# Ternary convolution stage: six pairs of x buffers, one padded image, loads five quarters ahead, and an accumulating DMA in place of an add

## The chip, the cores and the metric

The kernel is one program on one core of a Trainium2 chip. The metric is device time of that core in microseconds (us), taken as a median over runs. The engines that matter are TensorE (PE, matmuls), VectorE (DVE), ScalarE (ACT), GpSimd (POOL) and SyncE (SP). SP issues the DMAs that load, POOL issues those that store in the stage concerned. Each engine works through its own queue of instructions in order.

## The reference

Four layers act on x of shape (4, 256, 64, 64) in float32; each adds a convolution of the group-normalised x to x.

```
x = x + L0(gn(x))   # axial attention
x = x + L1(gn(x))   # 3x3 ternary convolution, 256 -> 256
x = x + L2(gn(x))   # two grouped binary 3x3 convolutions with shuffles
x = x + L3(gn(x))   # 3x3 convolution, 256 -> 256
# gn: 32 groups of 8 channels, mean and variance over channels of the group and 64x64
# L1: conv(x, ternize(w, 0.7) * alpha, padding 1) + bias
```

The result of layer 0 isn't formed as one tensor. The attention leaves two outputs in DRAM (called at_d[0] and at_d[1] in the program), each to be scaled per channel, with shifts that are constant per channel. The stage of layer 1 forms x + s0 * at_d[0] + s1 * at_d[1], takes its group statistics, normalises, convolves, and adds the convolution to it.

## The kernel before, in words

The work is one stage per layer. The change lies in the stage of layer 1, lines 1227 to 1418, whose tiles all carry names that begin with d.

**Tiling.** An image b (four of them) is held as two tiles t of 128 channels, and each tile is cut into four quarters q of 16 rows (128 partitions x 1024 elements). Two chunks per quarter compute the two output halves co. 16 quarters make 32 chunks.

**load(b, t, q)** (from L1264) takes a slot for the quarter in row_of (ten slots in five pairs, chosen by (q - b) % 5), issues an SP DMA for the input x into it (L145, in load_shuffled), then two SP DMAs for at_d[1] into a tile "a" (L1276). ACT scales that tile in place (L1279), DVE adds it into the slot (L1281), reading it with its elements in another order. Another SP DMA (L145) brings at_d[0] into another "a" tile, and a DVE scalar_tensor_tensor (L1284) scales and adds it into the slot, with the sum for the statistics as a by-product. ACT squares the slot for the other sum (L1262). There are three "a" buffers.

**norm(b, ts)** turns the sums of a whole image into a scale and a bias per channel: small DVE operations, tiny matmuls (L115, L125, L126) and an ACT operation (L106), one behind the other.

**transform(b, t, q)** writes the normalised quarter and one row of each neighbour into a padded image (ACT, L1322). Tile t has one padded image for interior quarters and one of 19 rows for the edge quarters 0 and 3, whose border rows were set to zero at the start. DVE forms four combinations of rows (L1324, L1328, L1329), ACT casts them to the high part (L1334), and DVE subtracts to get the low part (L1335). High and low parts are double-buffered over quarters.

**chunk(b, q, co)** does 48 matmuls of 128x128 by 128x512 (L1357): four row combinations, two input tiles, high and low part, three column shifts. ACT (L1372) and DVE (L1373, L1374, L1376) combine the four products into 16 rows, DVE adds them into the x slot with the sum for the next layer (L1381), ACT squares (L1262), and POOL issues the stores: x2_d for each chunk (L1386), and z_d for the second half (L1388).

**Order.** Image 0 is loaded and normed first. The loop over quarters then loads quarter q of the next image beside quarter q of this one, and norms the next image after its last quarter. The order on each engine isn't the order of the program text: a planner with priorities interleaves it, and within an engine the queue then runs in order. The next stage (L1420 and on) loads what was stored here, makes padded images (L1553) and row combinations e_tr (L1440), and convolves (L1451). Where a tile of that stage shares its place in SBUF with a tile of this one, it waits for it; the long string of names in the stage's pools sets which lies where.

Of the kernel before, what the change touches and what calls it, by code (L numbers as in the profile page):

```python
# [9 lines left out]
F32 = mybir.dt.float32  # L10
F32R = mybir.dt.float32r
BF16 = mybir.dt.bfloat16
AF = mybir.ActivationFunctionType
ALU = mybir.AluOpType
# [4 lines left out]
P = 128  # L19
B = 4  # L20
C = 256
HW = 4096
# [19 lines left out]
def network(ctx: ExitStack, tc, x, wqkv, relm, relt, relw, relv, counts, masks, vecs, rowv, ab, w1, l2w1, l2w2, l3w, mats, out):  # L42
# [4 lines left out]
    nc = tc.nc  # L47
# [40 lines left out]
    def pool(stack, name, bufs=1, space=None, side=None):  # L88
        kw = {"space": space} if space is not None else {}
        return stack.enter_context(tc.tile_pool(name=name, bufs=bufs, side=side, reuse_waits="tile", **kw))  # L90
# [75 lines left out]
    with ExitStack() as ph:  # L166
# [112 lines left out]
        for b in range(B):  # L279
            xs, gm, rs = ready  # L280
            qs = [qp.tile([P, 8, 8, 64], F32, name=f"qs{t}_{b}", tag="qs") for t in range(2)]
            for k in range(NB):
# [37 lines left out]
                if k % 2 == 1:  # L320
                    for r in range(2):
                        nc.scalar.dma_start(
                            out=vt_d[b][k // 2, r].rearrange("p a c m -> p a (c m)"),
# [8 lines left out]
                if k in (3, 7) and 2 * b + k // 4 - 1 in range(len(pieces)):  # L332
                    i = 2 * b + k // 4 - 1
# [410 lines left out]
    def from_scores(general, keep):  # L744
# [482 lines left out]
        with ExitStack() as ph:  # L1227
            ps_ = {
                k: pool(ph, f"d_{k}", {"a": 3, "o": 2}.get(k, 1))
                for k in "x2 x3 a x4 x5 x0 x6 p2 v0 h00 l00 u0 u1 x1 o s v1 h10 l10 h11 l11 p0 p1 p3 x7 x8 x9 h01 l01".split()  # L1230
            }
# [5 lines left out]

            pads = [
                ps_[f"p{i}"].tile([P, 18 + i // 2, 66], F32, name=f"d_pad{i}", tag="pad") for i in range(4)
            ]  # L1240
            u = [ps_[f"u{t}"].tile([P, 3, 4, C], F32R, name=f"d_u{t}", tag="u") for t in range(2)]
            for t in range(2):
                nc.vector.memset(pads[t][:, :, 0], 0.0)
                nc.vector.memset(pads[t][:, :, 65], 0.0)
                edge = pads[2 + t]
                nc.vector.memset(edge[:, 0:19:18, :], 0.0)
                nc.vector.memset(edge[:, 1:18, 0], 0.0)
                nc.vector.memset(edge[:, 1:18, 65], 0.0)

# [6 lines left out]
            def row_of(b, t, q):  # L1256
                xs[b, t, q] = ps_[f"x{2 * ((q - b) % 5) + t}"].tile([P, HW // 4], F32, name=f"dx_{b}_{t}_{q}", tag="x")
                return xs[b, t, q]
# [5 lines left out]
            def load(b, t, q):  # L1264
# [9 lines left out]
                for two in range(2):  # L1274
# [3 lines left out]
                    )  # L1278
                nc.scalar.activation(a, a, AF.Copy, scale=prs[t, 1][:, 0:1])  # L1279
                xv = xt.rearrange("p (n k i) -> p n k i", k=4, i=16)  # L1280
                nc.vector.tensor_tensor(xv, a.rearrange("p (k n i) -> p n k i", k=4, i=16), xv, ALU.add)  # L1281
                a = ap_.tile([P, HW // 4], F32, name=f"a0_{b}_{t}_{q}", tag="a")
# [26 lines left out]
            def transform(b, t, q):  # L1309


                nb, ra = norms[b, t]
                edge = q in (0, 3)
                pad = pads[2 + t if edge else t]
                pad = pad[:, 1:19] if q == 3 else pad[:, 0:18]
                parts = [(xs[b, t, q].rearrange("p (h w) -> p h w", w=64), slice(1, 17))]
# [88 lines left out]
            norm(0, slice(1, 2))  # L1405
            transform(0, 1, 0)
            for b in range(B):
                for q in range(4):
                    if b + 1 < B:
                        for t in range(2):  # L1410
                            load(b + 1, t, q)
                        if q == 3:
                            norm(b + 1, slice(0, 2))
                    nxt = (b, q + 1) if q < 3 else (b + 1, 0)
                    for co in range(2):
                        if nxt[0] < B:
                            transform(nxt[0], co, nxt[1])
                        chunk(b, q, co, b == q == co == 0)
            lost = None
            if not general:  # L1420
# [470 lines left out]
```

## Time and profile before

| what | value |
|---|---|
| time, median of 3 runs | 2771.07 us (2767.38 to 2775.86) |
| the profiled execution's own time | 2766.54 us |
| its span | 2764.8 us |
| mean granted TensorE clock | 0.937 |
| PE busy | 2398.3 us, 87% |
| DVE busy | 1980.3 us, 72% |
| ACT busy | 1205.8 us, 44% |
| POOL busy | 105.4 us, 4% |
| first matmul of the stage | 1485.0 us |
| last matmul of the stage starts | 1908.9 us |
| first matmul of the next stage's convolution | 1919.09 us |

The times of one execution come from its trace, in us from the span's start. A group line gives the line in the program, the engine, the operation, the output and input tiles, the count, then busy time and mean ns of one, and last the idle time of the engine just ahead of these instructions with what ended it ("<-"). SPq is the queue of DMAs that SyncE issues. A window line gives the busy time and the count of each engine in a stretch of time, then the granted clock, the share of the core's 16 DMA engines that was busy, and GB/s. Some matmul records can be missing from a trace, a few per cent.

### The profile page before, as it was taken

The numbers are of one execution on the slowest core, as the hardware profiler recorded it, in microseconds if no ns is written. First come the engines' busy times: TensorE is split into PE (matmuls) and PEld (weight loads), VectorE is DVE, ScalarE is ACT, GpSimd is POOL, SyncE is SP. The second block draws the span as 40 slices with busy tenths as digits, with TensorE's granted clock in tenths as the row PEclk, the third lists the DMA queues.
The fourth block names the chain that finished last, engine by engine and source line by source line (L and its number), as shares of the span: only waits on it lengthen the run. The fifth ranks groups of instructions, "written<-read, shape, count | busy, mean of one in ns | idle before, by whom it ended". The sixth has DMA issues, their size and how long they took to land.

```text
span 2764.8 us, 78125 instructions
## 1 busy us (share of the span) xinstructions
PE 2398.3 (87%) x34632; PEld 1576.4 (57%) x34632; DVE 1980.3 (72%) x3362; ACT 1205.8 (44%) x1984; POOL 105.4 (4%) x201
## 2 busy tenths in 40 slices
PE   7999788888997888888773998998979859999998
PEld 4566555556665666666662776776545424444443
DVE  6665788988775466666558788885888877967742
ACT  4555355555555544555435466553448421110100
POOL 0000100000001000000000000000000000000000
PEclk9999899999999888899886999999989979999999
DMA  6766366666667777778776546524337742324110
GB/s 239 258 201 205 89 190 163 172 168 186 155 150 159 244 251 249 256 242 274 232 234 220 186 154 201 189 101 158 126 128 265 288 159 91 138 105 137 46 42 36
DMA packets 287996, 489.87 MB, mean 177 GB/s; under 512 B 32736, under 2 KB 149088, under 8 KB 274848
## 3 DMA queue, kind: packets, MB, share of 16 engines
q1 hardware_dynamic: 224992, 359.52, 42.9%
q10 hardware_dynamic: 48256, 58.73, 6.2%
q0 software_dynamic: 14400, 66.53, 6.1%
q8 instruction: 273, 4.47, 0.7%
q14 instruction: 75, 0.61, 0.1%
HBM read 281.46 MB, written 203.23 MB: 175 GB/s over the span
## 4 chain that ended last, share of the span: by engine, by line
issue 38%; PE 30%; DVE 14%; DMA 11%; ACT 5%; POOL 1%; SPq 1%; DVEq 0%; ACTq 0%; POOLq 0%
PE pd L505 5%; PE dc L1357 4%; PE po L293 3%; PE pv L308 3%; PE pq L526 3%; DMA at_d<-o_False 2%; PE e_False L867 2%; DMA x<-x_d 2%; PE pr_False L936 2%; DVE pt L877 2%; PE pe_False L970 2%; DMA dx<-in_x 2%; PE den_False L918 2%; PE pa_False L945 2%; PE pc L1451 2%
## 5 line engine op out<-in xcount | busy, mean ns | idle before, releaser
L1066 PE MATMUL gc<-gtr,g_u 128*128 128x512 f32 x1152 | 503.4, 599 | 11.3 <-DVE gtr L1044 6.7
L1066 PEld LDWEIGHTS gc<-gtr,g_u 128*128 128x128 f32 x1152 | 219.3, 191 | 287.3 <-issue 269.4
L512 DVE STREAM_TRANSPOSE t<-pd 128x1024 f32<-128x1024 f32 x256 | 304.5, 1229 | 86.0 <-PE pd L505 80.7
L505 PE MATMUL pd<-rm,qb 64*32 64x256 f32 x8192 | 305.5, 389 | 41.4 <-DVE t L512 32.3
L1451 PE MATMUL pc<-e_tr,e_k 128*64 128x512 bf16 x2304 | 265.3, 391 | 20.5 <-DVE e_tr L1440 13.3
L532 ACT ACTIVATE o<-pq 128x512 f32<-128x512 f32 x256 | 150.6, 594 | 267.0 <-PE pq L526 264.8
L1357 PE MATMUL dc<-dh,d_u 128*128 128x512 f32 x768 | 233.5, 414 | 33.9 <-ACT dh L1334 33.8
L505 PEld LDWEIGHTS pd<-rm,qb 64*32 64x32 f32 x8192 | 168.4, 108 | 134.7 <-DVE t L512 57.4
L907 ACT ACTIVATE pt<-pt,sm 128x512 f32<-128x512 f32 x256 | 162.7, 710 | 174.9 <-DVE pt L877 174.8
L1357 PE MATMUL dc<-dl,d_u 128*128 128x512 f32 x768 | 229.3, 408 | 0.4 <-DVE dl L1335 0.2
L1451 PEld LDWEIGHTS <-e_k 128*64 128x64 bf16 x2304 | 145.5, 112 | 137.2 <-issue 28.9
L526 PEld LDWEIGHTS pq<-t,t 64*64 64x64 f32 x8192 | 146.0, 138 | 86.1 <-issue 71.6
L526 PE MATMUL pq<-t,t 64*64 64x64 f32 x8192 | 168.5, 225 | 28.6 <-issue 23.5
L1357 PEld LDWEIGHTS dc<-dh,d_u 128*128 128x128 f32 x768 | 148.6, 195 | 74.9 <-ACT dh L1334 35.8
L877 DVE TENSOR_TENSOR pt<-e_False,si_False 128x1024 f32<-128x1024 f32 x128 | 151.6, 1216 | 34.6 <-PE e_False L867 34.3
L1357 PEld LDWEIGHTS dc<-dl,d_u 128*128 128x128 f32 x768 | 145.7, 191 | 42.2 <-DVE dl L1335 4.1
L1084 ACT COPY gc_c<-gc 128x512 f32<-128x512 f32 x32 | 18.6, 582 | 344.0 <-PE gc L1066 344.0
L867 PE MATMUL e_False<-qc_False,rw 32*128 32x256 f32 x1024 | 131.1, 481 | 27.4 <-DVE pt L877 15.8
L538 ACT ACTIVATE sq<-o 128x1024 bf16<-128x1024 f32 x128 | 135.5, 1059 | 4.0
L293 PE MATMUL po<-xg,wt 128*128 128x512 f32 x256 | 120.8, 611 | 6.1 <-DVE st L300 4.5
L970 PE MATMUL pe_False<-pt,ve 128*32 128x64 f32 x4096 | 91.4, 244 | 39.9 <-issue 31.8
L308 PE MATMUL pv<-wt,xg 128*128 128x256 f32 x512 | 120.0, 382 | 0.0
(403 smaller groups left out, 3604.5 us busy)
## 6 DMA issues: line engine op xcount, KB each, us to landing
si_False<-qk_d SPq DMA_DIRECT2D x64, 1024.0 KB
qk_d<-o SPq DMA_DIRECT2D x496, 128.0 KB
x<-x_d SPq DMA_DIRECT2D x32, 1056.0 KB
xa<-in_x SPq DMA_DIRECT2D x16, 1024.0 KB
vt_d<-vs ACTq DMA_DIRECT2D x32, 512.0 KB
q_d<-qs SPq DMA_DIRECT2D x64, 256.0 KB
qb<-q_d SPq DMA_DIRECT2D x128, 128.0 KB
qc_False<-q_d SPq DMA_DIRECT2D x64, 256.0 KB
```

The costliest lines, as they stand in the source:

```text
L293: nc.tensor.matmul(psf, lhsT=wt[:, t, bass.ts(o, P)], rhs=xg[:, t, :], start=(t == 0), stop=(t == 1))
L308: nc.tensor.matmul(pv[:, j, :], lhsT=xg[:, t, pix], rhs=wt[:, t, C : 2 * C], start=(t == 0), stop=(t == 1),)
L505: nc.tensor.matmul(pds[t][32 * c : 32 * c + 32, m].rearrange("p j k -> p (j k)"), lhsT=q[rows, 2 * (gp % 2) + g, a, 32 * nb : 32 * nb + 32 ...
L512: nc.vector.transpose(ts[t][:, :, 32 * jh : 32 * jh + 32].rearrange("p a j b -> p j a b"), pds[t].rearrange("p m j k -> p j m k"),)
L526: nc.tensor.matmul(ps[nb][64 * g : 64 * g + 64, m, :], lhsT=ts[1][rows, n // 2, :, n % 2], rhs=ts[0][rows, n // 2, :, n % 2], start=True, ...
L532: nc.scalar.activation(o[:, :, n : n + 8, :], ps[nb].rearrange("p n (a b) -> p a n b", b=2), AF.Copy, accum_out=acc[:, nb, gp, col : col + 1],
L867: nc.tensor.matmul(es[x_ // 2][:, x_ % 2, :, :, par], lhsT=rw[rows, 63 - i : 127 - i].rearrange("p j r -> p (j r)"), rhs=q[rows, :, par, k ...
L877: nc.vector.tensor_tensor(dst, e, src, ALU.add)
L907: nc.scalar.activation(s, s, AF.Exp, scale=s2q[:, gp : gp + 1])
L1066: nc.tensor.matmul(ms[k], lhsT=u[t][:, dx, k, bass.ts(co, P)], rhs=vs[t][:, k, :, dx : dx + 64], start=(first and dx == 0), stop=(last and ...
L1357: nc.tensor.matmul(at[k], lhsT=u[t][:, dx, k, bass.ts(co, P)], rhs=v[:, k, :, dx : dx + 64], start=(first and p_ == 0 and dx == 0), stop=( ...
L1451: nc.tensor.matmul(m[64 * g : 64 * g + 64], lhsT=parts[:, g, i, k, dx, :], rhs=vs[g][:, k, 8 * (q % 2) : 8 * (q % 2) + 8, dx : dx + 64], s ...
```

## The change

Four things change together.

- The x slots become twelve in six pairs, chosen by (4b + q) % 6, so that the quarters of all images form one ring. To fit, the four padded images become two of 18 rows, one for each tile, which all quarters share; an edge quarter first sets its border row to zero with a DVE memset. The "a" buffers become four, and the tiles' order in SBUF is another.
- ACT no longer scales at_d[1] in place but writes another "a" tile, called ad, in the order that the slot has.
- The DVE add of that tile into the slot is gone. In its place POOL issues a DMA that adds ad into the slot (accum_op), SBUF to SBUF, 32 in all.
- The loop loads five quarters ahead: the first quarter of image 1 before the loop, then one tile of quarter n + 5 after each chunk of quarter n. The norm of the next image comes after its last quarter's load, one quarter earlier than before.

```diff
--- before.py
+++ after.py
@@ -1226,8 +1226,8 @@
 
         with ExitStack() as ph:
             ps_ = {
-                k: pool(ph, f"d_{k}", {"a": 3, "o": 2}.get(k, 1))
-                for k in "x2 x3 a x4 x5 x0 x6 p2 v0 h00 l00 u0 u1 x1 o s v1 h10 l10 h11 l11 p0 p1 p3 x7 x8 x9 h01 l01".split()
+                k: pool(ph, f"d_{k}", {"a": 4, "o": 2}.get(k, 1))
+                for k in "x2 x3 a x4 x5 x0 x6 p0 v0 h00 l00 u0 u1 x1 o s v1 h10 l10 h11 l11 x7 x8 x9 p1 x10 x11 h01 l01".split()
             }
             ap_, op, sp = ps_["a"], ps_["o"], ps_["s"]
             wide = pool(ph, "d_ps3", 1, PSUM)
@@ -1235,17 +1235,11 @@
             ring = [pool(ph, "d_ps", 2, PSUM)] * 2 + [wide]
             taken = [0]
 
-            pads = [
-                ps_[f"p{i}"].tile([P, 18 + i // 2, 66], F32, name=f"d_pad{i}", tag="pad") for i in range(4)
-            ]
+            pads = [ps_[f"p{t}"].tile([P, 18, 66], F32, name=f"d_pad{t}", tag="pad") for t in range(2)]
             u = [ps_[f"u{t}"].tile([P, 3, 4, C], F32R, name=f"d_u{t}", tag="u") for t in range(2)]
             for t in range(2):
                 nc.vector.memset(pads[t][:, :, 0], 0.0)
                 nc.vector.memset(pads[t][:, :, 65], 0.0)
-                edge = pads[2 + t]
-                nc.vector.memset(edge[:, 0:19:18, :], 0.0)
-                nc.vector.memset(edge[:, 1:18, 0], 0.0)
-                nc.vector.memset(edge[:, 1:18, 65], 0.0)
 
             def load_weights(t):
                 for dx in range(3):
@@ -1254,7 +1248,7 @@
             xs, vs, sums, mvs, norms, shift = {}, {}, {}, {}, {}, {}
 
             def row_of(b, t, q):
-                xs[b, t, q] = ps_[f"x{2 * ((q - b) % 5) + t}"].tile([P, HW // 4], F32, name=f"dx_{b}_{t}_{q}", tag="x")
+                xs[b, t, q] = ps_[f"x{2 * ((4 * b + q) % 6) + t}"].tile([P, HW // 4], F32, name=f"dx_{b}_{t}_{q}", tag="x")
                 return xs[b, t, q]
 
             def square(src, out):
@@ -1276,9 +1270,12 @@
                     nc.sync.dma_start(
                         out=a[two:P:2].rearrange("p (k f) -> p k f", k=4), in_=src[:, :, bass.ts(q, 256)]
                     )
-                nc.scalar.activation(a, a, AF.Copy, scale=prs[t, 1][:, 0:1])
-                xv = xt.rearrange("p (n k i) -> p n k i", k=4, i=16)
-                nc.vector.tensor_tensor(xv, a.rearrange("p (k n i) -> p n k i", k=4, i=16), xv, ALU.add)
+                ad = ap_.tile([P, HW // 4], F32, name=f"ad_{b}_{t}_{q}", tag="a")
+                nc.scalar.activation(
+                    ad.rearrange("p (n k i) -> p n k i", k=4, i=16), a.rearrange("p (k n i) -> p n k i", k=4, i=16),
+                    AF.Copy, scale=prs[t, 1][:, 0:1],
+                )
+                nc.gpsimd.dma_start(out=xt, in_=ad, accum_op=ALU.add)
                 a = ap_.tile([P, HW // 4], F32, name=f"a0_{b}_{t}_{q}", tag="a")
                 load_shuffled(a, at_d[0][b][bass.ts(t, P), bass.ts(q, HW // 4)], 0)
                 nc.vector.scalar_tensor_tensor(
@@ -1310,9 +1307,9 @@
 
 
                 nb, ra = norms[b, t]
-                edge = q in (0, 3)
-                pad = pads[2 + t if edge else t]
-                pad = pad[:, 1:19] if q == 3 else pad[:, 0:18]
+                pad = pads[t]
+                if q in (0, 3):
+                    nc.vector.memset(pad[:, 0 if q == 0 else 17, :], 0.0)
                 parts = [(xs[b, t, q].rearrange("p (h w) -> p h w", w=64), slice(1, 17))]
                 if q > 0:
                     parts.append((xs[b, t, q - 1][:, 15 * 64 :].rearrange("p (h w) -> p h w", w=64), slice(0, 1)))
@@ -1404,18 +1401,20 @@
             load_weights(1)
             norm(0, slice(1, 2))
             transform(0, 1, 0)
+            for t in range(2):
+                load(1, t, 0)
             for b in range(B):
                 for q in range(4):
-                    if b + 1 < B:
-                        for t in range(2):
-                            load(b + 1, t, q)
-                        if q == 3:
-                            norm(b + 1, slice(0, 2))
                     nxt = (b, q + 1) if q < 3 else (b + 1, 0)
+                    far = divmod(4 * b + q + 5, 4)
                     for co in range(2):
                         if nxt[0] < B:
                             transform(nxt[0], co, nxt[1])
                         chunk(b, q, co, b == q == co == 0)
+                        if far[0] < B:
+                            load(far[0], co, far[1])
+                    if far[0] < B and far[1] == 3:
+                        norm(far[0], slice(0, 2))
             lost = None
             if not general:
                 far = small(keep, [P, 1])
```

## The prediction

> **What bounds the kernel now.** I read the page's totals, then the stage of the ternary convolution (about 1485 to 1918 us, the only one edited) by 20 us windows, the timeline where a window is low, and last groups and SyncE waits.
>
> ```profile
> PE 2398.3 (87%) x34632; PEld 1576.4 (57%) x34632; DVE 1980.3 (72%) x3362; ACT 1205.8 (44%) x1984; POOL 105.4 (4%) x201
> ...
> q0 software_dynamic: 14400, 66.53, 6.1%
> ...
> L1357 PE MATMUL dc<-dh,d_u 128*128 128x512 f32 x768 | 233.5, 414 | 33.9 <-ACT dh L1334 33.8
> ```
>
> The convolution is 2 x 768 matmuls at L1357, 48 per chunk (one quarter, one output half), 32 chunks. Most of PE's idle time before them (33.8 us) is ended by ACT's cast L1334, the end of an input transform. Windows (PE busy and count, PEld, DVE, ACT, POOL, PE clock, DMA share, GB/s):
>
> ```profile
> 1480.00:1500.00 20.00, 10.44 (x30) 7.47 (x30) 19.86 (x22) 15.73 (x21) 0.00 (x0) 0.67 0.69 213
> 1500.00:1520.00 20.00, 7.28 (x20) 5.43 (x21) 14.91 (x31) 14.49 (x21) 0.00 (x0) 0.53 0.56 180
> 1600.00:1620.00 20.00, 14.10 (x50) 10.43 (x49) 17.29 (x32) 17.73 (x24) 1.06 (x2) 0.83 0.29 94
> 1620.00:1640.00 20.00, 20.00 (x87) 15.84 (x87) 17.77 (x29) 12.69 (x16) 0.53 (x1) 1.00 0.55 171
> 1700.00:1720.00 20.00, 12.54 (x49) 9.01 (x47) 18.33 (x44) 16.73 (x23) 1.06 (x2) 0.83 0.43 135
> 1800.00:1820.00 20.00, 14.00 (x53) 10.27 (x51) 16.42 (x42) 15.34 (x20) 1.59 (x3) 0.83 0.08 35
> ```
>
> Streaming, PE is the bound: 87 matmuls in 20 us, 0.230 us each, 11.0 us per chunk. At the three image boundaries only 50, 49 and 53 issue:
>
> ```profile
> 1608.53 2.50 PE L1357 MATMUL dc<-dh,d_u 128*128 128x512 f32 x5 [5.70 <-ACT dh L1334]
> ...
> 1712.88 2.93 PE L1357 MATMUL dc<-dh,d_u 128*128 128x512 f32 x6 [6.49 <-ACT dh L1334]
> ...
> 1814.44 2.92 PE L1357 MATMUL dc<-dh,d_u 128*128 128x512 f32 x6 [5.70 <-ACT dh L1334]
> ```
>
> These are three lines of the timeline; the bracket is PE's idle time and what ended it. The next image's statistics come after its last load: around 1594 the last L1284, then square, norm (1596.7 to 1601.7), pad and transform (1602.1 to 1608.5), while PE runs dry. Groups of the loads, window 1480 to 1910, and SyncE's waits, 1440 to 1920:
>
> ```profile
> L1284 DVE SCALAR_TENSOR_TENSOR dx<-a,sm,dx 128x1024 f32<-128x1024 f32 x28 | 35.9, 1282 | 0.2
> L1281 DVE TENSOR_TENSOR dx<-a,dx 128x1024 f32<-128x1024 f32 x28 | 34.3, 1224 | 19.4 <-issue 10.2 <-DMA dx<-in_x 8.3 <-ACT a L1279 0.7
> L1279 ACT ACTIVATE a<-a,sm 128x1024 f32<-128x1024 f32 x27 | 31.0, 1148 | 34.6 <-DMA a<-at_d 22.5 <-issue 12.0
> ```
> ```profile
> SPq L145 <- DVE dx L1281: 127.4, 23, 15.5
> ...
> SPq L145 <- DMA x_d<-dx: 46.4, 8, 16.8
> ...
> SPq L145 <- DMA z_d<-dx: 31.0, 10, 14.4
> ```
>
> An x load waits until the chunk that used its slot has stored the result (x_d, z_d). In the timeline, L1381 starts at 1641.38, the stores issue at 1642.90 and 1643.42, the x load at 1649.12, and the add L1281 starts at 1653.00: 11.6 us. For the other tile 1654.15, 1660.75, 1664.79: 10.6 us.
>
> **What the Trainium skill says.** "Collectives: The Full Stack", The bandwidth ceiling: the fold count and why AG ≠ RS ≠ AR: a DMA that adds needs two source reads, the addition itself is not the cost. "DMA: Bandwidth & Descriptors", Anatomy of one DMA, SWDGE path: about 2.0 us plus bytes at 436 GB/s; for 0.524 MB that is an estimate of 3.2 us, and x_d's landings here are 2.8 to 5.1, median 3.0 us, so it agrees. Twice the data term gives an estimate of 4.4 us for the accumulate; no trace of before has one. The same page, Issuing engines are not separate DMA queues: all issuers share 16 DMA engines. The trace's shares include every queue and allow such a sum.
>
> **The change part by part.**
>
> *Five quarters ahead, sixth pair.* The last quarter of the next image is loaded and normed one quarter (two chunks, 22 us) earlier. In the compiled order the norm's PE matmuls move from the last chunk before the boundary to three quarters through the one before it. Gain: three windows hold 152 matmuls, worth 152 x 0.230 = 35 us of their 60, so 25 us; the pure idle is 5.70 + 6.49 + 5.70 = 17.9, and the rest is slow restarting at clock 0.83. I take -24 (bounds -17.9, -25). Left over: at the first boundary the last load's L1284 stands in DVE's order only 7.3 us of work after the L1381 that frees its slot, ahead of the norm's operations; I estimate 4 us of PE stall there and at the second together (0 to 8).
>
> *DVE adds to DMAs.* 32 x 1.22 = 39 us of DVE work goes, 16 border memsets of about 0.1 us (128x66; nearest row, 128x1 at 0.15) come. Between first and last L1381 DVE has 312.9 us of work before and, with the trace's durations on the new order, 290.4 after: 9.7 per chunk instead of 10.4, against PE's 11.0. While PE streams that is worth nothing.
>
> *What the accumulate adds to the chain.* x load, ACT scale, accumulate, L1284 replace x load, add, L1284. From L1381 to L1284: 11.6 + about 0.6 issue (stores: 0.533) + landing 4.4 = 16.6 us. The order leaves on average 14.9 us of DVE work between the two (10.5 before to the add), which at PE's pace is 14.9 x 11.0 / 9.7 = 16.9 us. So it just fits. Beyond that each load stalls DVE, behind which the transforms and evictions queue, and PE waits for those: the chunk takes L / 1.54, as 14.9 / 9.7 = 1.54 chunks lie between. L = 17 costs nothing, 18 gives 11.7 us (+0.7), 19 gives 12.3 (+1.3), for 20 refills: 0, +14, +27 us. Single distances run from 7 to 20, so some stalls come even at 16.6; I take +5 (0 to +30).
>
> *POOL's queue.* It becomes store, accumulate, store, z store, accumulate. An accumulate waits there for the x load into the slot just stored, and the next chunk's store is queued behind; that store's slot waits in turn. One round is 9.4 + 0.5 for one tile and 10.3 + 0.5 for the other = 20.7 us, against 22.0 per quarter: hidden, with 1.3 us to spare. Longer landings come out of this margin, priced in the same +5.
>
> *DMA.* One copy of 0.524 MB costs q0's rate: 0.061 x 2764.8 x 0.524 / 66.53 = 1.33 us of all 16 engines. With two reads up to 2.7; two per 22 us quarter adds 0.12 to 0.24 to a share of 0.55 in the streaming window. Below full, so a lengthening only.
>
> *SP and ACT at the start.* The a0 load waits for the buffer of an earlier accumulate (four "a" buffers) and the next a1 stands behind it in SP's queue. For the second tile's norm (1502 us before) I estimate 3 us later; bounds +10, and -5 because DVE was 19.86 of 20 us busy in 1480 to 1500 and loses four adds of 1.22 there. ACT's permuted scale: same 1.15 us taken; if twice, ACT is at 12.69 of 20 while streaming and hides 32 x 1.15.
>
> *Shared pad.* Tile t's transforms already follow one another on ACT and DVE, so no new wait that binds: zero; if its readers were late, one pad copy (1.25 us) for each of 12 edge quarters inside the stream, which DVE's 1.3 us slack per chunk covers. Dropped setup memsets: hidden under the layer before.
>
> *Tail.* Tiles moved in SBUF: the next layer's first e_tr now lies over the last quarter's x tile and must wait for its stores (last issue 1913.86, z_d landing median 4.5, so about 1918.5) before its transform of 0.7 us pieces; PE restarted at 1919.09. I take +3 (1 to 6).
>
> Sum: -24 + 4 + 5 + 3 + 3 = -9. On the profiled execution (2766.54 us, span 2764.8) that is 2757.5; the median shown, 2771.07, is 4.5 above it, so I predict 2762 as median. Runs differ by 0.15% around it; 0.3%, 8.3 us, is what a measurement here can tell from no change.
>
> **Rivals.**
>
> *The accumulate sets the pace (slower).* Place: L1284 on DVE, waiting for a POOL DMA. For it: 16.6 against 16.9 us is no margin, DMA gets busier, POOL has 1.3 us. Against: a load now runs over three quarters before its transform, so only DVE's order, never missing data, can make PE wait, and distances average out. With 7 us landing L is 19.2, 12.5 us per chunk, 20 x 1.5 = +30, less the 24 saved, plus 10 elsewhere: 2771 + 16 = 2787. It decides for slower from L = 18.5 (12.0; +20 against the other -14, so +6) to 18.7 (above +8).
>
> *Full gain.* The accumulate lands like a store (3.2 us), DVE's freed time shortens start and boundaries: -24 + 0 - 2 + 1 + 2 = -23: 2748. For: the saturated start. Against: the first boundary's 7.3 us.
>
> *Boundaries only shifted.* If the last load's refill is late by the 10 us that a blocked POOL queue costs, norm comes late again and half of the 24 returns: -12 + 12 = 0, 2771. For: the norm sits behind L1284 in DVE's order. Against: it moved a whole chunk ahead.
>
> **How the numbers follow.** Forecast 0.44, of it 0.33 below 2763 and 0.11 above (own range 2752 to 2768); full gain 0.12; shifted 0.12 (0.10 same, 0.02 slower); accumulate pace 0.32 (0.31 slower, 0.01 same). So faster 0.45, same 0.22, slower 0.33. Range 2747 to 2790: it cuts about one in ten on each side.
>
> **What would show it.** Right: windows at the boundaries with over 75 matmuls; L1284 with idle time below 10 us ended by the accumulate; accumulate landings of 4 to 5 us. Wrong: L1284's idle over 20 us, POOL stores waiting for x loads longer than 2 us, streaming windows below 80 matmuls, or the first convolution chunk more than 10 us later.

## The result and the profile after

The change made the kernel slower: 2786.73 us median (2781.4 to 2793.16, 6 runs) against 2768.7 us (2760.02 to 2775.86, 6 runs); ratio 1.0062, 95% interval 1.004 to 1.0083. The profiled execution has a span of 2779.5 us, against 2764.8 before.

From the page after: the totals, the queue that POOL issues into, and the convolution's first group.

```profile
PE 2395.8 (86%) x34632; PEld 1582.8 (57%) x34632; DVE 1944.2 (70%) x3340; ACT 1204.8 (43%) x1984; POOL 133.5 (5%) x233
...
q0 software_dynamic: 19008, 83.31, 9.3%
...
L1354 PE MATMUL dc<-dh,d_u 128*128 128x512 f32 x768 | 235.0, 415 | 14.8 <-ACT dh L1331 14.3
```

The 33.8 us that PE stood before the convolution's matmuls waiting for ACT's cast have become 14.3, and DVE has 36 us less work. Both are what the change set out to do, and the kernel is slower. The windows of the stage (the same columns as before the change) show where PE stands now.

```profile
1540.00:1560.00 20.00, 20.00 (x85) 15.65 (x85) 11.34 (x17) 8.74 (x12) 1.50 (x3) 1.00 0.91 257
1560.00:1580.00 20.00, 19.49 (x82) 15.09 (x81) 15.75 (x24) 10.77 (x11) 3.38 (x5) 1.00 0.85 239
1580.00:1600.00 20.00, 7.82 (x33) 5.83 (x31) 7.27 (x18) 6.71 (x12) 2.85 (x4) 0.83 0.94 282
1600.00:1620.00 20.00, 19.37 (x73) 15.50 (x74) 15.34 (x38) 13.18 (x19) 1.44 (x2) 0.83 0.54 166
...
1700.00:1720.00 20.00, 13.01 (x46) 10.23 (x45) 8.18 (x28) 7.37 (x13) 2.80 (x4) 0.74 0.77 206
1800.00:1820.00 20.00, 17.27 (x64) 13.51 (x63) 13.15 (x41) 9.89 (x14) 1.06 (x2) 0.83 0.13 54
```

Away from the boundaries PE still issues 82 to 88 matmuls in most windows. The stalls are still three, one for each image, but they come earlier, and the DMA share just ahead of the first is 0.85 to 0.94. In the timeline after, they end at another instruction:

```profile
1600.63 0.59 PE L115 MATMUL pst<-sm,mt 128*128 128x2 f32 x2 [12.81 <-DVE sm L1295]
...
1709.50 0.59 PE L115 MATMUL pst<-sm,mt 128*128 128x2 f32 x2 [6.99 <-DVE sm L1295]
...
1808.26 0.59 PE L115 MATMUL pst<-sm,mt 128*128 128x2 f32 x2 [2.73 <-DVE sm L1295]
```

L115 is the first tiny matmul of norm. It stands in PE's queue inside a chunk, and PE takes its queue in order: all convolution matmuls behind it wait until the statistics of the next image are there, that is, until its last load is. Before the change, PE ran dry because the transform came late (17.9 us in all). Now it is held by the norm matmul (12.81 + 6.99 + 2.73 = 22.5 us), because the loads come late. Ahead of the first stall, POOL gets to an accumulate only when the x load has landed, and DVE then stands for that accumulate:

```profile
1589.05 0.87 POOL L1278 DMA_DIRECT2D dx<-ad  x1 [2.70 <-DMA dx<-in_x]
...
1591.10 1.28 DVE L1281 SCALAR_TENSOR_TENSOR dx<-a,sm,dx 128x1024 f32<-128x1024 f32 x1 [7.47 <-DMA dx<-ad]
```

Groups after (window 1470 to 1930) and SyncE's waits (1440 to 1940) show the loads of the whole stage:

```profile
L1281 DVE SCALAR_TENSOR_TENSOR dx<-a,sm,dx 128x1024 f32<-128x1024 f32 x28 | 35.9, 1283 | 69.8 <-DMA dx<-ad 46.1 <-issue 21.6 <-DMA a<-at_d 2.1
...
L1278 POOL DMA_DIRECT2D dx<-ad x28 | 24.3, 869 | 254.1 <-ACT ad L1274 89.6 <-DMA dx<-in_x 85.1 <-ACT dh L1331 21.9
```
```profile
SPq L1270 <- DMA dx<-ad: 85.2, 13, 8.6
SPq L145 <- DMA dx<-ad: 80.6, 13, 10.3
```

Three waits around the accumulate are visible: DVE's L1281 for its landing (46.1 us), POOL's own queue for the x load (85.1), and SyncE's loads for an "a" buffer that an accumulate still reads (85.2 + 80.6 = 166). They are called the slot chain, POOL's order and the ring below. The DMA view of the stream (1520 to 1850), first before and then after, gives the landings in us, last column.

```profile
x_d<-dx POOLq DMA_DIRECT2D x26, 512.0 KB, 3.0
...
z_d<-dx POOLq DMA_DIRECT2D x13, 512.0 KB, 4.7
```
```profile
x_d<-dx POOLq DMA_DIRECT2D x25, 512.0 KB, 5.3
dx<-ad POOLq DMA_DIRECT2D x22, 512.0 KB, 5.4
...
z_d<-dx POOLq DMA_DIRECT2D x12, 512.0 KB, 6.8
```

**Where the 15 us lie.** The chunks' last DVE step (L1381 before, L1378 after) gives three lengths from one line of each trace: when the first runs, how long from first to last, and how long from the last to the next layer's first convolution matmul (1919.09 us before, 1934.37 after). What follows that matmul takes 842 to 851 us in every trace of this study but doesn't belong to the change.

```profile
L1381 DVE SCALAR_TENSOR_TENSOR dx<-dc_o,dx x32: 1215/1221/1227, 1528.2 to 1911.8; 128x1024 f32<-128x1024 f32 x32
```
```profile
L1378 DVE SCALAR_TENSOR_TENSOR dx<-dc_o,dx x32: 1201/1219/1226, 1529.1 to 1923.5; 128x1024 f32<-128x1024 f32 x32
```

The first result is 0.9 us later, the stream of 383.6 us becomes 394.4 (+10.8), the tail of 7.3 becomes 10.9 (+3.6). The sum is 15.3.

The 0.9 us hide something. When the first chunk runs depends on when the layer before ends, too, and that scatters: its last store of at_d[1] (L985) is issued between 1441.0 and 1470.4 us in the twenty traces of this study, though no edit touches that layer. Before and after:

```profile
L985 ACTq DMA_DIRECT2D at_d<-o_False x32: 326/326/1017, 971.8 to 1459.4; - x32
```
```profile
L985 ACTq DMA_DIRECT2D at_d<-o_False x32: 326/326/920, 970.7 to 1446.3; - x32
```

From that store to the first L1381 or L1378 it is 68.8 us before and 82.8 after. This length, called the start below, repeats well: it is 82.8 and 83.0 us in two kernels with the same start (after, g3_start_only), and 66.6 and 66.4 in two others (e13_add_a3, e11_traffic), whose first chunks are 17.2 us apart. So inside the stage the start is 14.0 us longer, the stream 10.8 and the tail 3.6, which makes 28.4; the layer before happened to end 13.1 us earlier. The medians differ by 18 us. The lengths are of one execution each, so part of the 28.4 may be scatter.

### The profile page after: what moved, and what is told of

It is laid out like the page before. It is cut to its first block, busy times and chain, and to the rows that moved or that the text cites. A ratio compares the mean times of both kernels' runs of the same rounds, so it can differ in the third digit from the quotient of the medians.

```text
span 2779.5 us, 78149 instructions
## 1 busy us (share of the span) xinstructions
PE 2395.8 (86%) x34632; PEld 1582.8 (57%) x34632; DVE 1944.2 (70%) x3340; ACT 1204.8 (43%) x1984; POOL 133.5 (5%) x233
## 5 line engine op out<-in xcount | busy, mean ns | idle before, releaser
L1066 PE MATMUL gc<-gtr,g_u 128*128 128x512 f32 x1152 | 504.2, 600 | 11.1 <-DVE gtr L1044 6.7
L1450 PE MATMUL pc<-e_tr,e_k 128*64 128x512 bf16 x2304 | 264.8, 391 | 22.2 <-DVE e_tr L1439 12.1
L1354 PE MATMUL dc<-dh,d_u 128*128 128x512 f32 x768 | 235.0, 415 | 14.8 <-ACT dh L1331 14.3
L1450 PEld LDWEIGHTS <-e_k 128*64 128x64 bf16 x2304 | 154.2, 112 | 129.9 <-issue 29.6
L945 PE MATMUL pa_False<-pt,vb 128*32 128x64 f32 x4096 | 97.9, 235 | 22.7 <-issue 15.4
```

The costliest lines, as they stand in the source:

```text
L1066: nc.tensor.matmul(ms[k], lhsT=u[t][:, dx, k, bass.ts(co, P)], rhs=vs[t][:, k, :, dx : dx + 64], start=(first and dx == 0), stop=(last and ...
L1354: nc.tensor.matmul(at[k], lhsT=u[t][:, dx, k, bass.ts(co, P)], rhs=v[:, k, :, dx : dx + 64], start=(first and p_ == 0 and dx == 0), stop=( ...
L1450: nc.tensor.matmul(m[64 * g : 64 * g + 64], lhsT=parts[:, g, i, k, dx, :], rhs=vs[g][:, k, 8 * (q % 2) : 8 * (q % 2) + 8, dx : dx + 64], s ...
```

## The experiments

The table gives each run's ratio to the kernel before and, from its profile (one execution each), when the first chunk's last step runs, and the lengths of start, stream and tail, all in us.

| run | ratio, 95% interval | first | start | stream | tail |
|---|---|---|---|---|---|
| before | 1 | 1528.2 | 68.8 | 383.6 | 7.3 |
| after | 1.0062 (1.004 to 1.0083) | 1529.1 | 82.8 | 394.4 | 10.9 |
| e1_add | 0.9868 (0.9817 to 0.9919) | 1518.8 | 59.2 | 361.8 | 8.5 |
| e2_acc_only | 1.029 (1.0243 to 1.0337) | 1566.8 | 96.4 | 438.5 | 7.3 |
| e3_copy | 0.9968 (0.9934 to 1.0003) | 1532.7 | 73.9 | 373.0 | 10.8 |
| e4_norm_late | 1.008 (1.0063 to 1.0098) | 1533.5 | 80.8 | 390.8 | 11.2 |
| e5_ad_own | 1.0117 (1.0081 to 1.0152) | 1551.3 | 103.6 | 387.4 | 10.9 |
| e6_side | 1.0057 (1.0039 to 1.0075) | 1542.0 | 82.4 | 389.1 | 11.1 |
| e8_stores_act | 1.01 (1.0071 to 1.0128) | 1535.7 | 81.0 | 406.3 | 9.2 |
| e9_old_loop | 0.9841 (0.98 to 0.9883) | 1510.8 | 62.4 | 358.7 | 8.4 |
| e13_add_a3 | 0.9925 (0.9881 to 0.9968) | 1533.3 | 66.6 | 363.6 | 14.6 |
| e11_traffic | 0.9944 (0.9923 to 0.9966) | 1516.1 | 66.4 | 377.6 | 8.6 |
| e14_small | 0.9924 (0.9902 to 0.9946) | 1510.1 | 69.1 | 364.9 | 10.8 |
| e1b_add_ad | 0.989 (0.9846 to 0.9935) | 1517.6 | 66.5 | 369.4 | 9.1 |
| g1_ring5 | 1.0105 (1.0084 to 1.0127) | 1529.8 | 82.4 | 392.2 | 11.1 |
| g2_side5 | 1.006 (1.0032 to 1.0087) | 1542.5 | 80.2 | 387.4 | 10.9 |
| g3_start_only | 0.9964 (0.9942 to 0.9986) | 1539.1 | 83.0 | 358.9 | 8.2 |
| g4_add5 | 0.9883 (0.9854 to 0.9912) | 1508.9 | 57.0 | 366.1 | 8.3 |
| h1_ring5_act | 1.0149 (1.0111 to 1.0187) | 1535.5 | 83.2 | 401.9 | 8.9 |
| h2_side5_act | 1.0065 (1.0037 to 1.0093) | 1525.3 | 82.4 | 391.9 | 8.5 |

### Is it the accumulate? (e1_add, e2_acc_only, e4_norm_late)

e1_add keeps the whole change but the accumulating DMA (this diff is shortened; "permuted" stands for the reordered view):

```diff
-                ad = ap_.tile(..., tag="a")
-                nc.scalar.activation(ad (permuted), a (permuted), AF.Copy, scale=prs[t, 1][:, 0:1])
-                nc.gpsimd.dma_start(out=xt, in_=ad, accum_op=ALU.add)
+                nc.scalar.activation(a, a, AF.Copy, scale=prs[t, 1][:, 0:1])
+                nc.vector.tensor_tensor(xv, a.rearrange("p (k n i) -> p n k i", k=4, i=16), xv, ALU.add)
```

> The changed kernel with the accumulating DMA taken out: ACT scales the tile in place and DVE adds it into the slot, as before; six pairs, shared pads, four a buffers and loads five quarters ahead stay. Theory A (the accumulate in the chain from store to L1281 makes the last load of an image late, and PE's small norm matmuls wait for it): the three boundary stalls of 12.8, 7.0 and 2.7 us go, PE gaps of the stage below 3 us in all, and the time is 15 to 25 us below the kernel before, about 2748 us. Theory B (the earlier norm itself, or the store and load chain through six slots, stops PE whatever does the add): gaps over 8 us stay at the boundaries, time 2765 us or more.

e2_acc_only makes the opposite edit on the kernel before, and nothing else.

> The kernel before with nothing changed but the add: ACT writes a second a tile and POOL accumulates it by DMA; five pairs, four pads, three a buffers and the old loop stay. Theory A: the old loop has only 10.5 us of DVE work between freeing and refilling a slot, so each refill stalls DVE by about 16.6 - 12 = 4 us or more: 24 refills, +40 us or more at the most, at least +15 us, so 2785 to 2815 us. Theory B: the accumulate is hidden also here, within 6 us of the kernel before.

e4_norm_late keeps the accumulates and moves norm and the next image's first transform behind the first chunk of the last quarter:

```diff
+                        if q == 3 and co == 0:
+                            chunk(b, q, co)
+                            if nxt[0] < B:
+                                norm(nxt[0], slice(0, 2))
                         if nxt[0] < B:
                             transform(nxt[0], co, nxt[1])
-                        chunk(b, q, co, b == q == co == 0)
+                        if q < 3 or co == 1:
+                            chunk(b, q, co, b == q == co == 0)
...
-                    if far[0] < B and far[1] == 3:
-                        norm(far[0], slice(0, 2))
```

> The changed kernel with norm and the first transform of the next image put after the first chunk of an image's last quarter instead of ahead of it; accumulates stay. PE's small norm matmuls then stand at 7.0, 15.0 and 23.0 chunks instead of 6.6, 14.7 and 22.5, so 4.2, 3.0 and 5.3 us later. Theory A (the loads are late): the stall at the first boundary falls from 12.8 to about 9 us, at the second from 7 to 4, the third vanishes, unless the transform behind it is now late: 2776 to 2784 us. Theory B (placement alone): stalls gone, 2755 to 2768 us.

e1_add is 1.3% faster than the kernel before, more than theory A expected. e2_acc_only is 2.9% slower, 2856 us and so well beyond what either theory expected. So the accumulate, with the third tile ad that it needs, costs about (1.0062 - 0.9868) x 2769 = 54 us in the changed kernel and 80 us in the old one. By lengths, the changed kernel stands above e1_add by 23.6 us in the start, 32.6 in the stream and 2.4 in the tail. The windows of e1_add at the places where PE stood:

```profile
1580.00:1600.00 20.00, 20.00 (x86) 15.72 (x85) 17.76 (x33) 14.15 (x19) 0.53 (x1) 1.00 0.39 129
1600.00:1620.00 20.00, 20.00 (x89) 15.90 (x88) 18.05 (x37) 13.35 (x20) 1.59 (x3) 1.00 0.63 206
1680.00:1700.00 20.00, 17.15 (x71) 12.75 (x70) 19.91 (x34) 16.60 (x23) 1.05 (x2) 1.00 0.33 118
1780.00:1800.00 20.00, 18.84 (x81) 14.37 (x80) 20.00 (x29) 14.04 (x18) 1.05 (x2) 1.00 0.13 52
```

The first boundary is gone, the others lose 4 us of PE between them, the clock stays at 1.00. DVE is at 18 to 20 of 20 us here, with the adds still on it, and that costs little: the stream is 21.8 us shorter than before (361.8 against 383.6). e4_norm_late moved part of the stall from L115 (7.4 and 3.3 us) to the transform behind it (3.1 and 3.2) and gained nothing (1.008; its median of 2793 us is above what both theories gave). Where the norm stands is not the cause, so theory B of that run is out; late loads remain.

### Which other part of the change gains? (e9_old_loop, e13_add_a3, g4_add5)

e9_old_loop is e1_add with the loop of the kernel before:

```diff
-            for t in range(2):
-                load(1, t, 0)
...
+                    if b + 1 < B:
+                        for t in range(2):
+                            load(b + 1, t, q)
+                        if q == 3:
+                            norm(b + 1, slice(0, 2))
...
-                        if far[0] < B:
-                            load(far[0], co, far[1])
-                    if far[0] < B and far[1] == 3:
-                        norm(far[0], slice(0, 2))
```

> The run with the DVE add (six pairs, shared pads, four a buffers, no accumulate) with the loop of the kernel before: next image's quarter q loaded beside this one's, norm in the same quarter. In the compiled order PE's norm matmuls stand at 6.65, 15.3 and 22.9 chunks all the same. If the sixth pair of slots makes the loads early and the planner does the rest, within 6 us of the run with the new loop: 2730 to 2746 us. If the new loop's order makes the gain, the boundary stalls return in part: 2750 to 2770 us.

It is as fast (0.9841, stream 358.7). The last load is summed (L1278, the L1284 of before) 242.5 us after the first chunk's result, in e1_add 237.0 and before the change 271.8: the planner takes the loads ahead by itself. So the early loads and the vanished boundaries need no "five quarters ahead", which adds nothing that these runs can tell. They come with the six pairs and the shared pads that make room for them; no run separates these two, nor the new order of the tiles in SBUF.

e13_add_a3 is e1_add with three a buffers (`-{"a": 4` `+{"a": 3`).

> The run with the DVE add with three a buffers instead of four, as the kernel before had. If two tiles per load need no fourth buffer: within 6 us of it, 2728 to 2744 us; else up to 2760 us. It is also the control for the run with bare traffic.

g4_add5 is e9_old_loop with `{"a": 5}` and one buffer for the tile o.

> The candidate for a version faster than both: DVE add, six pairs, shared pads, the old loop, five a buffers and one o buffer. Four buffers against three went with 15 us. If a fifth still lets SyncE's queue run further ahead at the start and in the stream: 2720 to 2732 us; if four were enough: as the run with the old loop, 2728 to 2738 us; if the single o buffer binds: over 2745 us.

With three buffers the start takes 66.6 us, with four 59.2, and the stream is nearly the same (363.6 and 361.8). The fourth buffer's gain, 0.6% with intervals that overlap, lies in the start (7.4 us) and the tail (6.1) if it is real. A fifth, at the price of the second o buffer, gave nothing more: against e9_old_loop the start is 5.4 us shorter and the stream 7.4 longer.

### Bytes or waits? (e3_copy, e14_small, e11_traffic, e1b_add_ad, e6_side)

e3_copy is a plain copy in the same place with the same waits:

```diff
-                nc.gpsimd.dma_start(out=xt, in_=ad, accum_op=ALU.add)
+                nc.gpsimd.dma_start(out=xt, in_=ad)
```

> The changed kernel with the POOL DMA a plain copy instead of an accumulate, in the same place of every queue with the same waits; the input x is left out of the sum, since the copy overwrites it. If the second source read is what costs (DMA engines 75 to 94% busy in the stretches before the stalls): landings fall from 5.4 to about 3 to 4 us, the DMA share by about 0.12, and at least half of the 18 us goes: 2765 to 2778 us. If the cost is the chain and the queues themselves (POOL waits for the x load, SyncE for the a buffer, whatever the transfer's rate): 2780 to 2788 us.

About half of the 54 us goes ((1.0062 - 0.9968) x 2769 = 26 us). The landing falls from 5.4 to 4.1 us. Queue q0 was busy 7.7% of 2761.3 us here, 9.3% of 2779.5 after and 6.3% of 2733.0 in e1_add: one copy costs (212.6 - 172.2) / 32 = 1.3 us of all 16 DMA engines, one accumulate (258.5 - 172.2) / 32 = 2.7 us. (This is the time that the packets took, in this traffic; the percentages are rounded, so each figure is good to about 0.1 us.)

e6_side keeps the traffic and POOL's instructions, but aims the accumulate beside the sum:

```diff
-                nc.gpsimd.dma_start(out=xt, in_=ad, accum_op=ALU.add)
+                nc.gpsimd.dma_start(out=a, in_=ad, accum_op=ALU.add)
+                nc.vector.tensor_tensor(xt, ad, xt, ALU.add)
```

> The changed kernel with its accumulates aimed beside the sum: POOL accumulates ad into the a tile that ACT has read already (nothing reads it again), and DVE adds ad into the slot as in the run without accumulates. DMA traffic, POOL's instructions and the buffers held until landing stay; the slot and L1281 no longer wait for the accumulate, nor the accumulate for the x load. If the chain through the slot is the cost: within 15 us of the run with the DVE add, 2735 to 2750 us. If the DMA traffic and the held buffers are: 2760 to 2785 us.

No slot waits for an accumulate here, and the time is that of the changed kernel (1.0057). So L1281's wait, the largest wait of DVE in the profile after, is not needed for the loss. The held buffers aren't quite those of the changed kernel, though: here the a tile is held until the landing beside ad. SyncE waits 101.8 + 28.9 = 130.7 us for accumulates.

e14_small accumulates 16 of the 1024 columns, otherwise as e6_side:

```diff
-                nc.gpsimd.dma_start(out=a, in_=ad, accum_op=ALU.add)
+                nc.gpsimd.dma_start(out=a[:, 0:16], in_=ad[:, 0:16], accum_op=ALU.add)
```

> The run with the accumulate beside the sum, with 16 of the 1024 columns accumulated instead of all: every wait and held buffer stays, with the landing's fixed part alone (2 to 3 us), and 1/64 of the traffic. If the bytes are the cost: within 10 us of the run with the DVE add, 2730 to 2748 us. If the held buffers and the order of the queues are the cost whatever is moved: 2765 us or more.

e1b_add_ad has the third tile and DVE's add, and no DMA:

```diff
-                nc.gpsimd.dma_start(out=xt, in_=ad, accum_op=ALU.add)
+                nc.vector.tensor_tensor(xt, ad, xt, ALU.add)
```

> The changed kernel with three tiles per load in the ring of four a buffers as there, ad written by ACT, and DVE adding ad into the slot; no DMA in its place. Against the run with the DVE add it has only the third tile: if the ring with three tiles is tight by itself, 2750 us or more; if it is tight only because a tile is held until an accumulate lands, within 8 us of it, 2726 to 2746 us.

It gives 0.989 against 0.9868, with intervals that overlap; start and stream are 7.3 and 7.6 us longer. So the third tile alone may be worth some 6 us of the 54, and it is the nearer control for e6_side and e14_small.

e11_traffic is the run with three buffers and DVE's add (e13_add_a3), plus accumulates into an added scratch tile that nothing waits for:

```diff
                 nc.scalar.copy(hi, v)
+                if 1 <= 4 * b + q <= 11:
+                    nc.gpsimd.dma_start(
+                        out=scratch, in_=hi.rearrange("p k h w -> p (k h w)")[:, 0 : HW // 4].bitcast(F32), accum_op=ALU.add
+                    )
```

> The run with the DVE add and three a buffers, plus the traffic alone: after each input transform of quarters 1 to 11, POOL accumulates 512 KB of the high-part tile into a scratch tile that nothing reads, 22 in all (the changed kernel has 24 in the same stretch). No slot and no a buffer waits for it. If the second read's DMA time is the cost in itself (the other loads and stores land later): at least half of the 45 us that the changed kernel's stream loses against the run with the DVE add, so 2758 us or more. If buffers held until a landing are the cost: within 8 us of its control, 2728 to 2746 us.

The DMA views of the stream of e6_side, e14_small and e11_traffic, one line each:

```profile
a<-ad POOLq DMA_DIRECT2D x23, 512.0 KB, 6.2
```
```profile
a<-ad POOLq DMA_DIRECT2D x19, 8.0 KB, 3.5
```
```profile
d_scratch<-dh POOLq DMA_DIRECT2D x20, 512.0 KB, 5.8
```

Start, stream and tail together, which leaves out the scatter of the layer before:

| run | what of the accumulate it has | sum |
|---|---|---|
| e1b_add_ad | the third tile alone | 445.0 |
| e14_small | all but the slot chain, with 1/64 of the bytes | 444.8 |
| e3_copy | everything, as a copy | 457.7 |
| e6_side | all but the slot chain | 482.6 |
| after | everything | 488.1 |
| e13_add_a3 | nothing (control of the next) | 444.8 |
| e11_traffic | the bytes of 22, that nothing waits for | 452.6 |

An accumulate of 8 KB, with its issue on POOL and its place in every queue, costs nothing that these runs can tell; with 512 KB the same program takes 38 us more (37 by the ratios, 1.0057 and 0.9924). So the loss comes with the bytes. That doesn't yet say how. More bytes take more of the DMA engines, and they also land later (6.2 us against 3.5), so that buffers are held longer: SyncE waits 130.7 us for accumulates in e6_side and 59.2 + 19.2 = 78.4 in e14_small. e11_traffic has the bytes without the holding, though none at the start. Its stream is 14.0 us longer than its control's and its tail 6.0 shorter; the ratios, 0.9944 and 0.9925, are not distinguishable. Yet the DMA share is nearly the same: over the first 280 us of the stream it is 0.73 in e11_traffic, 0.74 in e6_side and 0.75 in the changed kernel, against 0.53 in e13_add_a3. So bytes that nothing waits for don't give the whole loss, and may give little of it.

### Which wait? (e5_ad_own, e8_stores_act, g1_ring5, g2_side5, h1_ring5_act, h2_side5_act)

Each of these is meant to ease one or more of the three waits. e5_ad_own gives ad a buffer of its own (the comment stands for the edit of the list of pools):

```diff
-                k: pool(ph, f"d_{k}", {"a": 4, "o": 2}.get(k, 1))
+                k: pool(ph, f"d_{k}", {"a": 3, "o": 2}.get(k, 1))   # and a pool "ad" of one
...
-                ad = ap_.tile([P, HW // 4], F32, name=f"ad_{b}_{t}_{q}", tag="a")
+                ad = ps_["ad"].tile([P, HW // 4], F32, name=f"ad_{b}_{t}_{q}", tag="ad")
```

> The changed kernel with the same four buffers split: three for the a tiles that SyncE's DMAs fill, one for the tile ad that the accumulate reads. SyncE then never waits for an accumulate (85 + 81 us of such waits in the profile after); ACT's scale waits for the accumulate before it instead. If the shared ring of a buffers carries the cost, SyncE's queue runs ahead and at least 10 us go: 2765 to 2778 us. If the cost is the transfer and the slot chain (L1281 waits for the landing), within 6 us of the changed kernel, 2781 to 2793 us, or slower where ACT is held up.

e8_stores_act issues both stores from ACT:

```diff
-                nc.gpsimd.dma_start(out=x2_d[b][bass.ts(co, P), cols], in_=xq)
+                nc.scalar.dma_start(out=x2_d[b][bass.ts(co, P), cols], in_=xq)
... (z_d likewise)
```

> The changed kernel with x_d and z_d stores issued by ACT, so that POOL's queue holds accumulates alone and no store stands behind one that waits for an x load (85 us of such waits after). If POOL's order is the cost: stores issue within 2 us of L1378, slots refill sooner, and at least 10 us go: 2765 to 2778 us. If it is the rate and latency of the accumulate itself: within 6 us of the changed kernel, 2781 to 2793 us.

g1_ring5 has five "a" buffers, with one o buffer to make room:

```diff
-                k: pool(ph, f"d_{k}", {"a": 4, "o": 2}.get(k, 1))
+                k: pool(ph, f"d_{k}", {"a": 5, "o": 2}.get(k, 1))
...
-                o = op.tile([P, 8, 2, 64], F32, name=f"{name}_o", tag="o")
+                o = op.tile([P, 8, 2, 64], F32, name=f"{name}_o", tag="o", bufs=1)
```

> The changed kernel with five a buffers instead of four (paid for by one buffer instead of two for the tile o, which DVE alone writes and reads). With five, a load's first a1 DMA waits for the accumulate two loads back, with four its a0 DMA waited for the one before. Theory ring (a tile held until the accumulate's bytes have landed stops SyncE's queue, and with it all later loads): SyncE's waits for the accumulate fall from 166 us to below 60 and at least half of the 53 us that the accumulate costs come back: 2762 us or less. Theory slot chain (L1281 waits for the landing, x loads for stores): within 8 us of the changed kernel, 2780 to 2795 us.

g2_side5 is e6_side with the same:

> The run with the accumulate beside the sum, with five a buffers as above. With four, its time was that of the changed kernel although no slot waited. Theory ring: now within 15 us of the run with the DVE add, 2735 to 2752 us. If the traffic at these instants or POOL's order is the cost: still 2770 us or more.

h1_ring5_act and h2_side5_act are these two with the stores on ACT as well:

> The changed kernel with two reliefs together that did nothing alone: five a buffers, and the stores issued by ACT so that POOL's queue holds accumulates alone. What is left of the accumulate's waits is the slot chain (x load, accumulate, L1281). If each of ring, POOL order and slot chain is enough by itself to make the last loads of an image late, this changes nothing either: 2782 to 2800 us. If ring and POOL order were the two that had to go together: 2745 to 2768 us.

> The same with the accumulate aimed beside the sum (into the a tile that ACT has read): five a buffers, stores on ACT, and no slot chain. All three waits are eased; the traffic stays. If the waits in parallel are the cost: within 15 us of the run with the DVE add, 2735 to 2752 us. If the accumulates' bytes are the cost where they fall (start and refills): 2765 us or more.

All stay at 1.006 to 1.015. In g1_ring5 SyncE's longest total is no longer the accumulate:

```profile
SPq L145 <- DMA x_d<-dx: 77.1, 10, 10.2
SPq L145 <- DMA z_d<-dx: 65.6, 9, 11.8
SPq L1270 <- DMA dx<-ad: 57.8, 9, 9.1
```

The waits for the accumulate fell from 166 us to below 60 as the ring theory wanted, the waits for stores rose in their place (from 22.2 + 29.3), and the stall at the first boundary was 15.08 us. So the ring alone isn't the cause. In e5_ad_own the wait only moves: ACT's scale now waits 57.6 us for the accumulate, which still reads the one ad buffer, and SyncE waits 112.4 us for ACT.

The last theory, that the three waits stand in for one another, stays untested. h2_side5_act was to ease all three, but there the accumulate holds two tiles of the ring until it lands, and five buffers don't make up for it. SyncE's waits in h2_side5_act:

```profile
SPq L1270 <- DMA a<-ad: 93.8, 13, 12.6
...
SPq L145 <- DMA a<-ad: 61.5, 11, 9.6
```

That is 155.3 us, nearly the 166 of the changed kernel (g2_side5: 80.4 + 64.1 = 144.5). So these two runs leave out the slot chain, h2_side5_act POOL's order as well, and keep the ring and the bytes. No run eases all three and keeps the bytes.

### Start or stream? (g3_start_only)

g3_start_only accumulates for the ten loads before the loop and adds on DVE for the others:

```diff
+                if 4 * b + q >= 5:
+                    nc.scalar.activation(a, a, AF.Copy, scale=prs[t, 1][:, 0:1])
+                    nc.vector.tensor_tensor(xv, a.rearrange("p (k n i) -> p n k i", k=4, i=16), xv, ALU.add)
+                else:
                     ... (the accumulate)
```

> The changed kernel with accumulates for the ten loads before the main loop alone, and scale in place with DVE add for the 22 loads inside the stream. The first convolution chunks after the second tile's norm started at 1515 us after and at 1508 in the run with the DVE add, so the start is worth about 7 us of the 53: 2738 to 2750 us. If the start is the larger part: 2765 us or more.

It is 0.0096 x 2769 = 27 us above e1_add, between the two bounds. Its start is 83.0 us, as in the changed kernel (82.8) and not as in e1_add (59.2); its stream is 358.9, as good as any. So the ten loads ahead of the stream carry the whole of the start's loss, 24 us, and the other 22 the 33 us of the stream. The 7 us that the expectation gave the start were read without regard to when the layer before had ended, 1446.3 us after and 1459.6 in e1_add.

## Why the prediction was wrong

I forecast 2762 us, and 2747 to 2790 as the range; the time was 2787, inside the range but slower than before where I had said faster. By the steps:

- **Boundaries, -24.** The mechanism and the size were right, for the change without its DMA: e1_add's stream is 21.8 us shorter than before's, and 4 us are left at its boundaries, though at the second and third and not, as I put it, at the first and second. I gave the credit to the five quarters and the sixth pair together; e9_old_loop shows that the five quarters aren't needed. In the changed kernel the gain is eaten at the same places.
- **DVE's freed adds, nothing.** In agreement: e1_add has them still, with DVE at up to 20.00 of 20 us in a window, and is faster than both.
- **What the accumulate adds to the chain, +5.** This is the step that failed. Measured against e1_add the stream is 32.6 us longer. I had the accumulate's cost in DMA time at the upper end (2.7 us, measured 2.7) and its effect on the share right (0.56 before, 0.75 after over the first 280 us of the stream, within the +0.12 to +0.24), and then took it as "below full, so a lengthening only". That was the error: lengthened loads were priced at nothing, and the last ones of an image came so late that PE stood 22.5 us at the norm. Of the landings in that sum, the accumulate's own was 5.4, not 4.4, after an issue of 0.87 and not 0.6, and x_d's, on which the x load waits, went from 3.0 to 5.3 us (z_d's from 4.7 to 6.8). With those, L is 11.6 + 2.3 + 0.9 + 5.4 = 20.2 us, for which my own formula had +27 us or more. The formula's chain isn't the proof, though: e6_side has no such chain, x_d lands there in 3.9 us, and the time is the same.
- **POOL's queue, hidden.** 85.1 us of its waits are for x loads, so it was not hidden. But taking the stores out of it (e8_stores_act) gained nothing, so this wait doesn't set the time alone.
- **Start, +3.** The second step that failed, by its size: +14.0 us, outside the bounds of -5 and +10. Without the accumulates the start would have been 9.6 us shorter than before (e1_add, 59.2 against 68.8); with them it is 23.6 longer than that, and g3_start_only shows that the ten accumulates ahead of the stream suffice for it. I had priced only the waits in SP's queue there.
- **Tail, +3.** +3.6.

The rival "the accumulate sets the pace" gave 2787 us, which is the time, by luck: its sum has 12.5 us per chunk over 20 refills and 10 us elsewhere. PE isn't slowed chunk by chunk, it stands mainly at three norm matmuls behind late loads, and DVE's L1281 need not wait for it to happen. My signs of it were there: L1281 idle for over 20 us (69.8), and, counted from the end of the layer before, a first chunk more than 10 us later. The place, 22.5 us of PE at L115, is that of the rival of shifted boundaries, which gave 2771.

**What stays open.** The loss comes with the accumulate and with its bytes, 24 us in the start and 33 in the stream. By which way the bytes cost it, these runs don't tell: traffic that nothing waits for cost 14 us of the stream in one execution, which the whole times don't confirm, and of the three waits the slot chain, POOL's order and part of the ring were eased one or two at a time without gain, never all together. That the accumulate is issued just when the same load's other transfers are in flight is an argument that no run tests.

## What to carry to other kernels

Before an add is moved from an engine to a DMA, price it twice: in the engine's time, where no gain showed here (e1_add keeps the adds and is the faster), and in the DMA engines' time against what the stage's other transfers need at that moment. The share of the DMA engines is not that price: at 0.73 to 0.75 the stream took 377.6 us where nothing waited for the accumulates (e11_traffic) and 394.4 in the changed kernel, where slots, buffers and later loads did. When single profiles are compared, count from the end of the layer before: its scatter of up to 29 us hid 13 of the 14 us that the start had lost. Of several edits that come together, run the one without the doubtful part: here six pairs, shared pads and a fourth "a" buffer with the add left on DVE give 0.9868 of the kernel before, with the old loop 0.9841 (2732 us), which beats both kernels.

## What the runs showed of the hardware

An accumulating DMA of 512 KB from SBUF to SBUF cost 2.7 us of all 16 DMA engines, a plain copy in the same place 1.3 us, so twice as much. It landed in 5.4 us (4.4 to 9.1) against 4.1 for the copy, and its issue kept POOL for 0.87 us, where the copy's took 0.54. An accumulate of 8 KB landed in 3.5 us. The Trainium skill, "Collectives: The Full Stack", The bandwidth ceiling: the fold count and why AG ≠ RS ≠ AR, explains a ratio of two in collectives by the second source read that an add needs; for this DMA the ratio is measured here, the reason isn't.
